# Three hand-written orders of steps laid out anew in a graph-attention kernel

## The chip, the cores and the metric

The kernel runs on one core of one Trainium2 chip. The core has a matrix engine (TensorE; PE in the profile, its weight loads PEld), a vector engine (VectorE, DVE), a scalar engine (ScalarE, ACT), GpSimd (POOL) and a queue that issues transfers (SP). Each engine takes its own instructions in their order; semaphores tie the engines together. The metric is the time of one execution on the device in microseconds, the median of several runs.

## The reference

64 independent graphs of 256 nodes with 512 features each, all in float32, and two layers, each with a residual:

```python
h = jnp.maximum(_layernorm(x, axis=-1), 0.0)
x = x + _L0_gnn_ref(adj, h, W1, att_src1, att_dst1, b1, W2, att_src2, att_dst2, b2)
h = jnp.maximum(_layernorm(x, axis=-1), 0.0)
x = x + _L1_gnn_ref(h, adj, W_proj, W_att, b_att)
```

Layer 0 is two graph attentions with an ELU between them (four heads of 256, then one head of 512), layer 1 is one attention with eight heads of 64 and a ReLU. One attention is

```python
xl = (x @ W).reshape(B, N, H, F)
e = jax.nn.leaky_relu(asrc[:, :, None, :] + adst[:, None, :, :], 0.2)
e = jnp.where(mask[..., None], e, NEG_INF)
attn = jax.nn.softmax(e, axis=1)
out = jnp.einsum('bsdh,bshf->bdhf', attn, xl)
```

where `asrc` and `adst` are dot products of a node's features with two attention vectors.

## The kernel before

**Stages of a graph.** A `Graph` object (from L292) has one method a step. `load` brings x and the adjacency; `masks`, `caps` and `cap3` make the masks of the layers (`cap3` transposes one by two transfers); `bias` adds b2 on GpSimd. `stats1`, `norm1` normalise; `away1` writes h to DRAM and reads it back permuted, and `turn1` finishes its transposition on VectorE and lets GpSimd form four sums (`left`). Then the first projection (`m1a`, `m1b`, two halves of the columns), `exp1`, `rows1`, four `edges1`, four `gat1` (head pair, row block), `out1`, `elu1`. `send2` and `back2` transpose half of the result over DRAM and VectorE, `turn2` the other half on TensorE; second projection `m2`, `exp2`, `rows2`, `edges2`, two `gat2`, `out2`. Layer 1: `stats3`, `norm3`, `turn3` (transposes on TensorE, copies on ScalarE, sums on GpSimd), projection `m3`, `exp3`, `rows3`, eight `edges3`, four `gat3`, `out3`, then `range` and `store`.

**Products.** A projection is a Strassen-like product (L38) of seven block products, `p1` to `p7`, here in the order their operands come; `c22` adds up one block of the result. The first product needs only a block of the input as it is; `p5`, `p6`, `p7`, `p4` need the sums that GpSimd makes (`left`, L212) and the sums of the weights (`right`, L551).

**Attention.** `exp` takes exponentials of the node terms, `rows` (`spread`, L233) transposes them on VectorE, writes them to DRAM and reads them back spread over all partitions (one transfer for `rows2`, two for `rows1`, four for `rows3`, after one small write). `edges` (`weigh`, L286) makes the 256 x 256 weights of one head: per row block a scaling on ScalarE and one operation on VectorE. `gat` is the matmul with the weights; its last column gives the sum by which `out` divides. `gat1` (L394) and `gat2` (L466) use 128-wide weights; `gat3` (L518) issues per head, row block and half 64-wide weights against 65 columns, 16 source matmuls a step, 32 records in the profile.

**The order.** Nothing is scheduled automatically: `run` (L693) goes through a text of steps and issues each, so a text is the order on every engine and queue at once. An item is the graph's offset from the round r, the step and its arguments; items of graphs outside 0 to 63 are left out. `head` runs once, `order` for r = 2 to 62, `tail` once with r = 64. In the order before, round r starts with the `gat1` of graph r and carries parts of the graphs r-2 to r+2; the head ends inside graph 2, with the load of graph 3 last.

**Weights.** The steps `w` of the head prepare weights once: `dots1`, `dots2` (eight steps of four dot products each, L559, on VectorE) and `dots3` (a product on GpSimd, a reduction on VectorE, L629) make the columns for the attention terms; `sums1`, `sums2`, `sums3` the sums of the weights. A product of `m1a` needs the columns that `dots1` writes into `w1a_sb`; `m1b` has none.

**Buffers.** PSUM: four of `ps_mm` (tile pm), two of `ps_sum`, two of `ps_tr`. Nine of e, three of wy, two each of xs, ad, cap and mask, one of h.

```python
    for r in range(2, B - 1):
        run(order, r)
    run(tail, B)
```

Of the kernel before, what the change touches and what calls it, by code (L numbers as in the profile page):

```python
# [97 lines left out]
def short_path(ctx, tc, flags, x, adj, w1, att_src1, att_dst1, b1, w2, att_src2, att_dst2, b2, w_proj, w_att,  # L98
# [487 lines left out]
    class Weights:  # L586
# [49 lines left out]


    head = """
        w dots1 3, w dots1 0, 0 turn0, 0 masks, 0 m1b p1, w dots1 2, w dots1 5, w sums1 1, w dots1 1, 0 m1b
        p2, 0 m1b p6, 0 m1b p7, w dots2 0, 0 m1b p5, w dots1 4, 0 m1b c22, w dots1 6, w dots1 7, 0 m1b p4, 0  # L640
        m1a p1, w sums1 0, 0 m1a p6, w dots2 3, 0 m1a p7, w dots2 2, w dots2 7, w dots2 5, 0 m1a p5, 0 bias,
        0 m1a p2, 0 m1a c22, w dots2 1, 0 m1a p3, 0 m1a p4, w dots2 4, w dots2 6, w columns2, 0 m1b p3, w
        sums2 0, w sums2 1, 0 exp1, 0 rows1, w sums2 2, 0 caps, w sums2 3, 0 edges1 0, 0 edges1 3, 0 edges1
        1, 0 edges1 2, 0 gat1 0 0, w load3, 0 cap3, 0 out1 0 0, 0 gat1 0 1, 0 out1 0 1, 0 gat1 1 0, 0 elu1 0
        0, 0 send2 0, 0 out1 1 0, 0 elu1 0 1, 1 load, 0 send2 1, 0 elu1 1 0, 0 gat1 1 1, 0 back2 0, 0 out1 1
        1, 0 back2 1, w dots3 7, 1 stats1, 1 masks, 0 elu1 1 1, 1 norm1, w dots3 1, 0 m2 p1, w dots3 2, w
        dots3 0, 1 away1, w dots3 6, 0 turn2 0, 0 turn2 1, w dots3 5, 0 m2 p6, w dots3 4, w dots3 3, 1
        turn1, w sums3 0, w sums3 1, 0 m2 p2, w sums3 2, 0 m2 p7, 0 m2 p5, 1 m1a p1, 0 m2 p4, 1 m1a p6, 0 m2
        c22, 0 m2 p3, 1 m1a p7, 1 m1a p5, 0 exp2, 0 rows2, 1 m1a c22, 1 m1b p1, 1 bias, 1 m1a p4, 1 m1a p3,
        1 m1a p2, 1 exp1, 1 rows1, 1 m1b p6, 1 m1b p2, 1 m1b p5, 0 edges2, 1 m1b p7, 1 caps, 0 gat2 0, w  # L650
        sums3 3, 1 m1b c22, 0 out2 0, 0 stats3 0, 1 edges1 0, 1 m1b p3, 0 gat2 1, 1 edges1 1, 0 out2 1, 1
        m1b p4, 1 edges1 2, 1 gat1 0 0, 1 out1 0 0, 0 stats3 1, 2 load, 1 gat1 0 1, 1 out1 0 1, 1 elu1 0 1,
        1 edges1 3, 0 norm3, 1 elu1 0 0, 1 cap3, 1 send2 0, 1 gat1 1 0, 0 turn3, 1 send2 1, 1 out1 1 0, 1
        gat1 1 1, 1 out1 1 1, 2 stats1, 0 m3 p1, 0 m3 p2, 1 elu1 1 0, 1 elu1 1 1, 2 norm1, 1 back2 0, 0 m3
        p6, 0 m3 p5, 1 turn2 0, 1 back2 1, 0 m3 p7, 2 away1, 1 m2 p1, 2 bias, 2 masks, 1 turn2 1, 0 m3 c22,
        1 m2 p2, 0 m3 p4, 0 m3 p3, 0 exp3, 0 rows3, 2 turn1, 1 m2 p6, 1 m2 p5, 1 m2 p7, 2 m1a p1, 1 m2 c22,
        1 m2 p3, 2 m1a p6, 1 m2 p4, 1 exp2, 1 rows2, 0 edges3 1, 2 m1a p5, 2 m1a p7, 2 m1a c22, 0 edges3 2,
        0 edges3 4, 2 m1b p1, 2 m1a p3, 0 edges3 3, 2 m1a p2, 0 edges3 6, 0 edges3 0, 2 m1b p6, 0 gat3 0 1,
        2 m1a p4, 2 m1b p2, 2 exp1, 2 rows1, 2 m1b p5, 0 edges3 5, 0 gat3 0 0, 0 edges3 7, 1 edges2, 2 m1b
        p7, 0 out3 0 0, 0 out3 0 1, 1 gat2 0, 2 caps, 2 m1b c22, 1 out2 0, 1 stats3 0, 2 edges1 0, 2 m1b p3,  # L660
        2 edges1 1, 2 edges1 3, 2 m1b p4, 1 gat2 1, 1 out2 1, 3 load
    """
# [28 lines left out]
    weights = Weights()

# [293 lines left out]
```

## Time and profile before

| | |
|---|---|
| median of 3 runs | 3147.14 us (3146.95 to 3150.41) |
| span of the profiled execution | 3144.0 us |
| TensorE busy | 3064.8 us, 97% |
| PEld, VectorE, ScalarE, GpSimd busy | 84%, 78%, 60%, 40% |
| DMA, mean | 110 GB/s |
| VectorE busy, 0 to 100 us, 100 to 200 us | 69.64 us, 68.66 us |
| VectorE busy, 200 to 300 us | 80.27 us |

"Busy" is the union of the times in which an engine has an instruction. A matmul's end is modelled and matmuls overlap, so on TensorE a full row can still hold short waits; the distance between two starts shows them. In a line of the timeline the first number is the start from the span's beginning in microseconds, the second the busy time, then engine, source line, operation, what is written and read, the shape, and how many instructions were merged; in brackets the idle time before it and what ended it. GpSimd's times are rough.

### The profile page before, as it was taken

What the parts mean: (1) busy time and instruction counts of PE and PEld (TensorE: products, weight loads), DVE (VectorE), ACT (ScalarE), POOL (GpSimd) and SP (SyncE); (2) the same over time, 40 slices, a digit from 0 to 9 for tenths busy, and PEclk for the clock granted to TensorE, in tenths of its full rate; (3) what the DMA queues carried; (4) which work ended last, traced back from release to release, by engine and by line L of the source; (5) the groups of instructions that cost most, each with busy time, mean ns of one, the idle gap of its engine ahead of it and who ended that gap; (6) DMA issues with size and microseconds to landing.
All of it is one profiled execution on the core that took longest, in us unless ns stands there. A gap on an engine that the chain in (4) does not pass through costs nothing. (4 is left out here: it accounts for less than half of the span.)

```text
span 3144.0 us, 60657 instructions
## 1 busy us (share of the span) xinstructions
PE 3064.8 (97%) x21312; PEld 2628.9 (84%) x21312; DVE 2466.5 (78%) x6503; ACT 1882.1 (60%) x4743; POOL 1245.5 (40%) x1434
## 2 busy tenths in 40 slices
PE   4899999999999999999999999999999999999997
PEld 3788888888888888888888888888888888888886
DVE  7588788787787787787787887887887877877875
ACT  2466666665666666566566666566666656666664
POOL 1443433433433434434434434434434334334342
PEclk8999999999999999999999999999999999999999
DMA  4234443333433433434433333433444334334331
GB/s 138 71 110 113 117 107 115 118 108 105 126 102 111 127 102 111 127 100 113 120 106 112 116 106 114 115 109 117 108 116 117 107 109 123 105 108 127 102 112 36
DMA packets 350779, 346.49 MB, mean 110 GB/s; under 512 B 78600, under 2 KB 236168, under 8 KB 350472
## 3 DMA queue, kind: packets, MB, share of 16 engines
q1 hardware_dynamic: 349096, 340.45, 37.6%
q8 instruction: 174, 2.85, 0.4%
q10 hardware_dynamic: 1376, 2.10, 0.2%
q14 instruction: 133, 1.09, 0.1%
HBM read 231.87 MB, written 102.20 MB: 106 GB/s over the span
## 5 line engine op out<-in xcount | busy, mean ns | idle before, releaser
L289 ACT ACTIVATE wy<-bc,exs_sb 128x256 f32<-128x256 f32 x1646 | 731.7, 500 | 261.7 <-DVE e L290 148.3
L260 DVE TENSOR_TENSOR xl<-pm,kept 128x256 f32<-128x256 f32 (+2 forms) x768 | 318.1, 421 | 414.6 <-PE pm L54 395.5
L60 ACT ACTIVATE kept<-sum 128x264 f32<-128x264 f32 (+3 forms) x768 | 294.4, 383 | 419.1 <-PE sum L54 416.2
L394 PE MATMUL pm<-xl,e 128*128 128x257 f32 x2048 | 498.6, 387 | 20.6 <-DVE e L290 15.1
L528 POOL TENSOR_TENSOR x<-x,o 128x256 f32<-128x256 f32 x256 | 196.4, 768 | 788.8 <-DVE o L526 770.2
L54 PE MATMUL sum<-w_sb,h1s 128*128 128x257 f32 x2048 | 489.7, 381 | 7.7 <-POOL h1s L216 7.1
L290 DVE SCALAR_TENSOR_TENSOR e<-wy,exs_sb,cap 128x256 f32<-128x256 f32 x1024 | 446.9, 479 | 56.0 <-ACT wy L289 56.0
L394 PEld LDWEIGHTS pm<-xl,e 128*128 128x128 f32 x2048 | 369.3, 190 | 100.2 <-PE pm L394 28.3
L54 PEld LDWEIGHTS sum<-w_sb,h1s 128*128 128x128 f32 x2048 | 380.6, 191 | 67.1 <-POOL h1s L216 7.5
L54 PE MATMUL pm<-w_sb,h1s 128*128 128x257 f32 x1536 | 365.4, 380 | 1.2 <-DVE xl L260 1.0
L181 POOL TENSOR_TENSOR rstd<-ve,neg_half 128x2 f32<-128x2 f32 x128 | 116.8, 912 | 622.0 <-DVE ve L179 622.0
L54 PEld LDWEIGHTS pm<-w_sb,h1s 128*128 128x128 f32 x1536 | 291.1, 190 | 45.4 <-issue 1.4
L290 DVE SCALAR_TENSOR_TENSOR e<-wy,exs_sb,mask 128x256 f32<-128x256 f32 x640 | 302.4, 523 | 5.2 <-ACT wy L289 5.2
L518 PEld LDWEIGHTS pm<-xl,e 128*64 128x64 f32 x8192 | 250.6, 138 | 47.3 <-issue 22.7
L54 PE MATMUL sum<-w1b_sb,hs 128*128 128x256 f32 x1024 | 266.7, 384 | 7.8 <-DVE w1b_sb L554 5.0
L54 PE MATMUL sum<-w1a_sb,hs 128*128 128x260 f32 x1024 | 268.7, 385 | 5.7 <-DVE w1a_sb L554 3.3
L54 PE MATMUL sum<-wp_sb,hs 128*128 128x264 f32 x1024 | 270.6, 387 | 3.0 <-ACT kept L60 2.5
L518 PE MATMUL pm<-xl,e 128*64 128x65 f32 x8192 | 269.2, 224 | 3.9 <-DVE e L290 2.9
L404 DVE SCALAR_TENSOR_TENSOR z<-pm,r,b_sb 128x256 f32<-128x256 f32 x512 | 247.8, 484 | 18.2
L466 PE MATMUL pm<-xl,e 128*128 128x257 f32 (+1 forms) x1024 | 242.6, 380 | 1.3 <-DVE e L290 1.3
L407 ACT ACTIVATE ez<-z 128x512 f32<-128x512 f32 x256 | 159.8, 624 | 125.0 <-DVE z L404 125.0
L54 PEld LDWEIGHTS sum<-w1b_sb,hs 128*128 128x128 f32 x1024 | 196.7, 193 | 36.9 <-issue 7.0
(103 smaller groups left out, 5076.3 us busy)
## 6 DMA issues: line engine op xcount, KB each, us to landing
bc<-kept SPq DMA_DIRECT2D x380, 256.0 KB
xs<-in_x_dram SPq DMA_DIRECT2D x64, 512.0 KB
out_dram<-x SPq DMA_DIRECT2D x64, 512.0 KB
kept_h<-h SPq DMA_DIRECT2D x63, 512.0 KB
h<-kept_h SPq DMA_DIRECT2D x63, 512.0 KB
kept_z<-z SPq DMA_DIRECT2D x124, 256.0 KB
z<-kept_z SPq DMA_DIRECT2D x124, 256.0 KB
ad<-in_adj_dram SPq DMA_DIRECT2D x64, 256.0 KB
```

Of the source, the lines that this page charges most:

```text
L54: self.nc.tensor.matmul(to[:, :self.n], self.lhs[:, i, c, :], self.rhs[:, i, c, :], start=(first and c == 0), stop=(last and c == self.nk ...
L60: self.nc.scalar.activation(s[:, :self.n], self.sum[:, :self.n], AF.Copy)
L181: nc.gpsimd.tensor_tensor(rstd, ve[:, 0, :], neg_half, ALU.pow)
L260: nc.vector.tensor_tensor(dst, pm, add, ALU.add)
L289: nc.scalar.activation(wy, bc, AF.Copy, scale=yw)
L290: nc.vector.scalar_tensor_tensor(dst, wy, xw, mask, ALU.max, op)
L394: nc.tensor.matmul(pm[:, :Q + 1], self.e[1, h][:, s, t * P:(t + 1) * P], xl1[:, s, h, L1:], start=(s == 0), stop=(s == T - 1))
L404: nc.vector.scalar_tensor_tensor(z[:, sl], pm[:, :Q], r, b1_sb[:, sl], ALU.mult, ALU.add)
L407: nc.scalar.activation(ez, z[:, 2 * g * F1:2 * (g + 1) * F1], AF.Relu, scale=-1.0)
L466: nc.tensor.matmul(pm[:, :n], self.e[2][:, s, t * P:(t + 1) * P], xl2[:, s, half, L2:L2 + n], start=(s == 0), stop=(s == T - 1))
L518: nc.tensor.matmul(pv[q:q + 64, h, :], self.e[3, a * G + h][:, s, t * P + q:t * P + q + 64], xl3[:, s, a * G + h, :], start=(s == 0), stop ...
L528: nc.gpsimd.tensor_tensor(to, to, o.rearrange("p h k -> p (h k)"), ALU.add)
```

## The change

The three texts are replaced; `Graph` gets an initial value for `bc2` and `bc3`, the rows that `rows2` and `rows3` set. Steps, instructions and buffers stay as they are. The round now begins with `edges1 3` of graph r-1 and carries parts of the graphs r-3 to r; the head ends inside graph 1, and the tail carries what is left of the graphs 60 to 63. The line numbers after the first hunk are higher by one.

```diff
@@ -295,6 +295,7 @@
         def __init__(self, b):
             self.b = b
             self.pms = {}
+            self.bc2 = self.bc3 = None
 
         def load(self):
             self.xs = io.tile([P, T, D], F32, name="xs")
@@ -636,57 +637,57 @@
     head = """
-        w dots1 3, w dots1 0, 0 turn0, 0 masks, 0 m1b p1, w dots1 2, w dots1 5, w sums1 1, w dots1 1, 0 m1b
-        p2, 0 m1b p6, 0 m1b p7, w dots2 0, 0 m1b p5, w dots1 4, 0 m1b c22, w dots1 6, w dots1 7, 0 m1b p4, 0
-        m1a p1, w sums1 0, 0 m1a p6, w dots2 3, 0 m1a p7, w dots2 2, w dots2 7, w dots2 5, 0 m1a p5, 0 bias,
-        0 m1a p2, 0 m1a c22, w dots2 1, 0 m1a p3, 0 m1a p4, w dots2 4, w dots2 6, w columns2, 0 m1b p3, w
-        sums2 0, w sums2 1, 0 exp1, 0 rows1, w sums2 2, 0 caps, w sums2 3, 0 edges1 0, 0 edges1 3, 0 edges1
-        1, 0 edges1 2, 0 gat1 0 0, w load3, 0 cap3, 0 out1 0 0, 0 gat1 0 1, 0 out1 0 1, 0 gat1 1 0, 0 elu1 0
-        0, 0 send2 0, 0 out1 1 0, 0 elu1 0 1, 1 load, 0 send2 1, 0 elu1 1 0, 0 gat1 1 1, 0 back2 0, 0 out1 1
-        1, 0 back2 1, w dots3 7, 1 stats1, 1 masks, 0 elu1 1 1, 1 norm1, w dots3 1, 0 m2 p1, w dots3 2, w
-        dots3 0, 1 away1, w dots3 6, 0 turn2 0, 0 turn2 1, w dots3 5, 0 m2 p6, w dots3 4, w dots3 3, 1
...
+        w dots1 2, w dots1 1, w dots1 3, w dots1 0, w dots1 7, w dots1 6, w dots1 4, 0 turn0, w dots1 5, w sums1 0,
+        0 m1a p1, 0 m1a p2, 0 m1a p6, w sums1 1, w dots2 0, 0 bias, 0 m1b p1, 0 m1a p5, 0 m1a p7, 1 load, 0 m1b p5,
+        0 m1a c22, 0 m1a p4, w dots2 7, 0 m1a p3, 0 exp1, 0 masks, 0 rows1, w dots2 3, w dots2 4, w dots2 1,
+        w dots2 2, 0 m1b p6, 0 caps, 0 m1b p7, 0 m1b c22, 1 stats1, 0 edges1 0, 0 m1b p4, 0 m1b p3, 0 edges1 1,
+        0 m1b p2, 0 edges1 3, 0 edges1 2, 0 gat1 0 1, 0 gat1 0 0, 0 out1 0 1, 1 norm1, 0 send2 0, 0 out1 0 0,
+        0 gat1 1 1, w dots2 6, 0 gat1 1 0, 0 elu1 0 1, 0 out1 1 0, 0 elu1 0 0, 0 back2 0, 0 send2 1, 0 out1 1 1,
+        w dots2 5, w columns2, 0 elu1 1 1, 0 elu1 1 0, w load3, 0 back2 1, w dots3 4, 0 cap3, 0 m2 p1, 0 turn2 0,
+        w dots3 7, w sums2 0, 1 away1, w sums2 1, w sums2 2, 1 bias, w dots3 3, 0 turn2 1, 0 m2 p2, 1 turn1,
+        w sums2 3, 0 m2 p5, 0 m2 p6, 1 m1a p1, 0 m2 p7, 1 masks, 0 m2 c22, 1 m1a p6, w dots3 6, 0 m2 p4, w dots3 1,
+        0 m2 p3, 0 exp2, 1 m1a p7, 1 m1a p5, 0 rows2, w dots3 2, 1 m1a c22, w dots3 0, 1 m1a p2, w dots3 5,
+        1 m1a p3, 1 caps, w sums3 0, 1 m1a p4, 1 exp1, 1 m1b p1, 1 rows1, w sums3 1, 1 m1b p5, 0 edges2, 1 m1b p6,
+        0 gat2 0, w sums3 2, 0 out2 0, 0 gat2 1, 0 stats3 0, 0 out2 1, 1 cap3, 1 edges1 0, 1 m1b p7, 0 stats3 1,
+        1 edges1 1, 1 edges1 2, 1 m1b p4, 0 norm3, 1 gat1 0 0, 1 out1 0 0, 1 m1b c22, w sums3 3, 1 m1b p2,
+        1 elu1 0 0
     """
     order = """
-        0 gat1 0 0, 0 edges1 2, 0 out1 0 0, -2 gat3 1 1, 0 cap3, -1 stats3 1, -2 gat3 1 0, -1 norm3, -2 out3
-        1 1, 0 gat1 0 1, 0 elu1 0 0, 0 out1 0 1, 0 gat1 1 0, -1 turn3, 0 out1 1 0, 0 gat1 1 1, 0 elu1 0 1,
-        -1 m3 p1, 0 out1 1 1, 0 elu1 1 0, 0 send2 0, 1 stats1, -1 m3 p5, -1 m3 p6, 0 elu1 1 1, 0 back2 0, 0
-        send2 1, -2 out3 1 0, -1 m3 p2, 1 norm1, 1 away1, 0 back2 1, -2 store, -1 m3 p7, 0 turn2 0, 0 turn2
-        1, 0 m2 p1, -1 m3 p4, -1 m3 c22, 0 m2 p2, -1 m3 p3, 0 m2 p6, 1 masks, -1 exp3, 1 caps, 0 m2 p5, 1
-        bias, -1 rows3, 0 m2 p7, -2 range, 1 turn1, 1 m1a p1, 0 m2 p4, 0 m2 c22, 0 m2 p3, -1 edges3 1, 0
-        exp2, 0 rows2, 1 m1a p6, -1 edges3 0, 1 m1b p1, -1 edges3 5, 1 m1a p7, 1 m1a p5, 1 m1a c22, -1
-        edges3 4, 1 m1a p2, -1 edges3 2, 1 m1a p4, 1 m1a p3, -1 edges3 3, 1 exp1, 1 m1b p6, 1 rows1, -1
-        edges3 7, -1 gat3 0 0, -1 gat3 0 1, -1 out3 0 0, 0 edges2, -1 edges3 6, 1 m1b p5, -1 out3 0 1, 1 m1b
-        p7, 1 m1b c22, 1 m1b p2, 0 gat2 0, 0 out2 0, 0 stats3 0, 1 edges1 0, 1 m1b p3, 1 edges1 1, 1 m1b p4,
-        0 gat2 1, 0 out2 1, 1 edges1 3, 2 load
+        -1 edges1 3, -1 gat1 0 1, -2 turn3, -3 out3 1 1, -1 out1 0 1, -1 m1b p3, -2 m3 p1, 0 load, -1 gat1 1 0,
+        -1 gat1 1 1, -1 out1 1 0, -1 send2 0, -1 elu1 0 1, -2 m3 p6, -1 out1 1 1, 0 stats1, -2 m3 p5, -2 m3 p7,
+        -1 send2 1, -1 back2 0, 0 norm1, -1 elu1 1 1, -1 elu1 1 0, -3 gat3 1 0, -2 m3 p4, -2 m3 c22, -2 m3 p2,
+        -1 back2 1, -1 turn2 0, -1 turn2 1, 0 masks, -2 m3 p3, 0 away1, -3 range, -2 exp3, -1 m2 p1, -2 rows3,
+        0 caps, -3 out3 1 0, 0 turn1, -1 m2 p5, -1 m2 p6, -1 m2 p2, -1 m2 p7, -1 m2 c22, 0 m1a p1, -2 edges3 1,
+        -2 edges3 3, -1 m2 p4, -1 m2 p3, -1 exp2, 0 m1a p6, -1 rows2, -2 edges3 0, 0 bias, -3 store, 0 m1a p5,
+        -2 edges3 7, 0 m1a p7, 0 m1a c22, -2 edges3 2, 0 m1a p2, -2 edges3 5, 0 m1a p4, 0 m1a p3, -1 edges2,
+        -2 gat3 0 0, 0 exp1, 0 m1b p1, -2 out3 0 0, 0 rows1, -1 gat2 0, -2 edges3 6, -1 out2 0, -1 gat2 1,
+        -2 edges3 4, -1 stats3 0, -1 out2 1, 0 m1b p6, -1 stats3 1, -2 gat3 0 1, 0 edges1 0, 0 m1b p7, 0 m1b p2,
+        0 edges1 1, 0 edges1 2, -1 norm3, 0 m1b p4, 0 gat1 0 0, 0 out1 0 0, 0 m1b p5, -2 out3 0 1, 0 m1b c22,
+        0 elu1 0 0, 0 cap3, -2 gat3 1 1
     """
     tail = """
...
-        edges3 2, 0 m1b p5, -2 edges3 4, 0 exp1, 0 m1b p2, -2 edges3 6, -2 gat3 0 0, -2 gat3 0 1, 0 m1b p6,
-        -2 out3 0 1, 0 m1a p2, -2 range, -1 edges2, -2 edges3 7, -2 edges3 5, -1 gat2 0, 0 rows1, 0 m1a c22,
-        -1 out2 0, -1 gat2 1, -1 stats3 0, -2 gat3 1 0, -1 out2 1, -1 stats3 1, -1 norm3, -1 turn3, -2 out3
-        0 0, -2 gat3 1 1, -1 m3 p1, -2 out3 1 1, 0 m1a p4, -1 m3 p2, -1 m3 p5, -1 m3 p6, -1 m3 p7, -1 m3 p4,
-        -1 m3 c22, -2 out3 1 0, -1 m3 p3, -1 exp3, -1 rows3, -1 range, -1 edges3 4, -1 edges3 6, -1 edges3
-        1, -1 edges3 0, -1 edges3 3, -1 edges3 2, -1 edges3 5, -1 edges3 7, -2 store, -1 gat3 0 0, -1 gat3 0
-        1, -1 gat3 1 1, -1 out3 0 1, -1 gat3 1 0, -1 out3 0 0, -1 out3 1 1, -1 out3 1 0, -1 store
...
+        -2 m3 p2, -3 gat3 1 1, -3 range, -2 m3 p5, -3 out3 1 1, -1 turn2 0, -1 turn2 1, -2 m3 p7, -3 store,
+        -2 m3 c22, -1 m2 p1, -2 m3 p3, -2 m3 p4, -2 exp3, -1 m2 p6, -1 m2 p5, -1 m2 p7, -2 rows3, -1 m2 c22,
+        -2 edges3 1, -1 m2 p2, -2 edges3 3, -2 edges3 5, -4 range, -2 edges3 0, -1 m2 p3, -2 edges3 6, -1 m2 p4,
+        -1 exp2, -1 edges2, -1 gat2 0, -1 gat2 1, -2 edges3 2, -1 out2 0, -1 stats3 0, -1 out2 1, -2 gat3 0 1,
+        -1 stats3 1, -2 gat3 0 0, -2 edges3 7, -2 edges3 4, -2 out3 0 0, -2 gat3 1 0, -1 norm3, -1 turn3,
+        -2 out3 1 0, -1 m3 p1, -2 range, -2 gat3 1 1, -1 m3 p6, -1 m3 p2, -1 rows2, -1 m3 p7, -1 m3 p5, -1 m3 p4,
+        -1 m3 c22, -1 m3 p3, -1 exp3, -2 out3 0 1, -2 out3 1 1, -1 edges3 6, -2 store, -1 edges3 5, -1 edges3 4,
+        -1 edges3 7, -1 edges3 0, -1 edges3 3, -1 edges3 1, -1 gat3 1 1, -1 edges3 2, -1 gat3 1 0, -1 gat3 0 1,
+        -1 out3 1 0, -1 out3 1 1, -1 out3 0 1, -1 gat3 0 0, -1 out3 0 0, -1 range, -1 store
     """
```

## The prediction

> **What bounds it now.** I read the totals first, then the stretches, then TensorE's own order of events, and last the waits at the start. The chain of waits on the page reaches back over less than one per cent of the span, so it carries nothing here.
>
> ```profile
> span 3144.0 us, 60657 instructions
> PE 3064.8 (97%) x21312; PEld 2628.9 (84%) x21312; DVE 2466.5 (78%) x6503; ACT 1882.1 (60%) x4743; POOL 1245.5 (40%) x1434
> ```
>
> ```profile
> 0.00:100.00 100.00, 53.93 (x191) 41.33 (x192) 69.64 (x226) 25.12 (x55) 32.34 (x45) 0.86 0.38 115
> 100.00:200.00 100.00, 92.55 (x539) 77.72 (x538) 68.66 (x180) 57.05 (x147) 34.36 (x41) 1.00 0.35 102
> 200.00:300.00 100.00, 99.82 (x743) 86.00 (x742) 80.27 (x211) 63.26 (x163) 38.55 (x44) 1.00 0.38 109
> ...
> 3100.00:3144.00 44.00, 27.63 (x334) 22.19 (x332) 23.07 (x73) 16.26 (x42) 9.30 (x14) 0.89 0.07 26
> ```
>
> The columns are stretch, length, busy time of PE, PEld, DVE, ACT and POOL, granted clock, DMA share, GB/s. TensorE is idle 53.5 us in the first 200 us (46.1 and 7.4), 16.4 us in the last 44, and 0.2 in a hundred between. So the rounds are bound by TensorE, and a new order can win there only what hides inside "busy": matmuls overlap, so I go by the distance from one start to the next.
>
> ```profile
> 155.15 1.89 PE L54 MATMUL pm<-w1b_sb,hs 128*128 128x256 f32 x8
> 156.97 1.15 PE L518 MATMUL pm<-xl,e 128*64 128x65 f32 x32
> 158.06 1.13 PE L54 MATMUL sum<-w1b_sb,hs 128*128 128x256 f32 x4
> 159.02 1.89 PE L466 MATMUL pm<-xl,e 128*128 128x257 f32 x8
> ```
>
> ```profile
> 1009.57 1.03 PE L54 MATMUL sum<-w1b_sb,hs 128*128 128x256 f32 x4
> 1010.52 2.09 PE L518 MATMUL pm<-xl,e 128*64 128x65 f32 x64
> 1012.54 1.13 PE L54 MATMUL pm<-w1b_sb,hs 128*128 128x256 f32 x4
> 1013.51 1.03 PE L54 MATMUL sum<-w1b_sb,hs 128*128 128x256 f32 x4
> 1014.37 1.03 PE L54 MATMUL pm<-w1b_sb,hs 128*128 128x256 f32 x4
> ...
> 1020.42 1.90 PE L394 MATMUL pm<-xl,e 128*128 128x257 f32 x8
> 1022.25 2.09 PE L518 MATMUL pm<-xl,e 128*64 128x65 f32 x64
> 1024.26 4.06 PE L394 MATMUL pm<-xl,e 128*128 128x257 f32 x16
> 1028.16 1.04 PE L196 MATMUL pt<-ident,h 128*128 128x128 f32 x8
> ```
>
> Each line gives a start and a busy time; one source matmul of the wide kind is two records. Four wide records take 0.86 us (1013.51 to 1014.37), eight 1.73, wherever they stand; an m2 product 1.74, an m3 product 0.89. The reader is to see two things. First, a run of the 64-wide matmuls of `gat3` has edges: before the run at 156.97, eight records take 1.82 us instead of 1.73, and after it four take 0.96 instead of 0.86. Second, the sixteen records from 1024.26 take 3.90 us, where sixteen take 3.46 and the edge 0.10: the other 0.33 us is a wait inside `gat1 1 0`, behind a VectorE that runs `out1`, `stats3` and `out3` without a break from 1022.97 to 1029. The round is 47.51 us long (a run begins at 202.86 and, 17 rounds on, at 1010.52).
>
> **The change, part by part: the runs of gat3.** No instruction is added, so TensorE's work could only change at edges. The round before has `gat3 0 0, gat3 0 1` and `gat3 1 1, gat3 1 0` side by side on TensorE (the steps between the last two do not use it). The round after has all four apart: `gat3 0 0` between `m1a p3` and `m1b p1`, `gat3 0 1` between `m1b p6` and `m1b p7`, `gat3 1 1` between `m1b p5` and the next round's `gat1 0 1`, `gat3 1 0` between `m3 p7` and `m3 p4`. Counting the instructions as built, runs of 64-wide matmuls rise from 129 to 251: 122 more. The price: two runs of 32 cost 2 x (0.09 + 1.09 + 0.10) = 2.56 us, one run of 64 costs 0.09 + 2.02 + 0.11 = 2.22. A split costs 0.34 us, and nothing hides it, as it is on the engine that sets the end. 122 x 0.34 = 41.5 us. The row at 156.97 is the only undisturbed single run. From below: the outer edges alone, 0.20 a split (24 us). From above: the other single run of the start, from 152.90 to 154.17, which holds a wait of its own, in place of one of the two: 0.09 + 1.27 + 0.12 + 1.28 - 2.22 = 0.54 (66 us). I take 0.34, as the outer edges of the long runs agree with the row.
>
> The Trainium skill ("TensorE: Matmul & The Clock Gate", Part 3, the span model) gives packed small matmuls about 4 ns of issue each and prices no edge; Part 2 there says that weight loads are pulled ahead of running matmuls. By it the 122 splits would cost about half a microsecond, an estimate from that page, and the sum below would be some 41 us lower. The row shows the edge, and the row decides.
>
> **The wait that goes.** In the new round `m1b p3` and `m3 p1` (0.86 + 0.89 us of TensorE) stand between `gat1 0 1` and `gat1 1 0`, and `stats3` has moved ahead of the round's end, so VectorE's work ahead of `out1 0 1` is `edges1 3` (0.80) and `out3 1 1` (0.55) against 2.6 us of `gat1 0 1` and `turn3`. The 0.33 us should go: 61 rounds x 0.33 = 20 us less. If it stays, add those 20 back.
>
> **The waits that come.** A cover has got thinner at `gat2 0`. Its e comes over `m2 p3`, `exp2`, `rows2`, DMA, `edges2`. In the old order two `gat3` and some ten products lie between; in the new one only six m1a products, `gat3 0 0` and `m1b p1`: 6 x 0.88 + 1.28 + 0.86 = 7.4 us. The chain: eviction 0.4, exponentials 0.4, the transpose and DMA 5.7, weighing 1.3, together 7.8. The 5.7 is from these rows:
>
> ```profile
> 1058.40 0.20 DVE L237 STREAM_TRANSPOSE wt<-exs_sb 128x32 f32<-128x32 f32 x1
> ...
> 1064.12 1.30 ACT L289 ACTIVATE wy<-bc,exs_sb 128x256 f32<-128x256 f32 x3 [1.67 <-DMA bc<-kept]
> ```
>
> That is `rows1`, with two transfers; `rows2` has one of half the size, so 5.7 is its upper side, and what it saves is unknown. TensorE keeps order: all behind `gat2 0` waits with it, `gat2 1` first, and on VectorE `out2 0`. Next, `gat1 0 0`: from the end of `gat2 0` TensorE has `gat2 1`, four m1b products and `gat3 0 1`, 1.73 + 3.44 + 1.28 = 6.45 us, while VectorE has `out2` twice (2.1), `edges3 4` (0.8), `stats3` (1.95), one eviction (0.35) and `edges1 0, 1` (1.6) = 6.8 us and may start 0.7 us earlier, at the first half of `gat2 0`: 0.35 us to spare. `m2 p5` wants the first sum that GpSimd makes after `turn2`'s copies, which queue on ScalarE behind `norm1` as in the old round; to spare, about nothing. On SP `cap3` now waits for the last `edges3` of two graphs earlier (two buffers of cap), and the load behind it for `cap3`; 8.6 us of TensorE's steps to the round's end and 8 more to `stats1`, less 2.5 for `cap3`, leave the load 14 us, and the first load of the program (issued at 0.80, used at 6.79) took 6. `away1`'s two transfers may hold VectorE at `turn1` (write and read took 7.4 us there: issued at 1037.29, used at 1044.66) with a microsecond left before `m1a p1`. So per round 0 to 0.8 us; I take 0.25, near the first of these waits: 61 x 0.25 = 15 us.
>
> **The start.**
>
> ```profile
> 11.65 0.43 DVE L559 CUSTOM_DVE_ANT_0 wy<-w1b_sb,x 128x256 f32<-128x256 f32 x1 [2.88 <-DMA w1b_sb<-in_L_gnn_W_dram]
> ...
> 19.72 2.55 DVE L559 CUSTOM_DVE_ANT_0 wy<-w1a_sb,x 128x256 f32<-128x256 f32 x1
> 22.20 2.86 DVE L554 TENSOR_TENSOR w1b_sb<-w1b_sb 128x512 f32<-128x512 f32 x4
> ```
>
> A dot starts every 0.35 us, but every 0.87 beside GpSimd's `left` and 2.5 beside `bias`. The new head puts all 32 of `dots1` first: 11.65 + 18 dots up to 22.2 (as the rows run) + 14 x 0.35 = 27.1 us to the first m1a product, where m1b began at 15.7. That is 11 us later, in a time in which TensorE mostly waited. Afterwards only 24 of 32 `dots2` come before `edges1`, and neither `columns2` nor `sums2`: 27.1 + sums1 5.7 + dots2 8.3 + evictions, masks and stats1 about 4.5 + waits 1.5 = 47 us, where `edges1` began at 57.95. And TensorE's 3.2 us before 74.64 and 7.1 before 82.75, the latter behind GpSimd with ten of `dots3`'s sixteen products ahead of `left`, shrink: now six of them stand ahead. To the end of the new head VectorE has 64 dots (22.2 us), the subtractions (14.1), `dots3` (5.6), graph 0's steps (19.7) and graph 1's (11.5), 73 us, and TensorE 51 (m1 23.5, m2 12.2, `gat1` 8.6, `gat2` 3.5, turns 2.9); from 11.65 on, with 5 us of slowing by GpSimd, that ends at 90 us at the earliest and leaves TensorE idle for 39, against 53.5. I take 10 us won, between 0 (the late first product costs all) and 15.
>
> **The end.** After the last `gat2` the chain over `norm3`, m3, `exp3`, eight `edges3`, `out3` and the store is the same; four rather than two `gat3` of the graph before fill it (2 us), and two more `edges3` stand ahead of `norm3` on ScalarE (2 x 0.8 us). I take nothing, plus or minus 3.
>
> **Sum** against the profiled span: 3144.0 + 41.5 - 20 + 15 - 10 = 3170.5 us. The median of the runs shown is 3147.1, 3.1 above that span; with that, 3174 us.
>
> **Rivals.** *The round gets waits of a microsecond.* For it: margins of 0.35 and 0 us, and VectorE's pieces cost up to twice as much beside GpSimd, as `bias` does at 19.72. Against: VectorE is 80% busy and catches up each round. At 1.0 us a round: 3147.1 + 41.5 - 20 + 61 - 10 = 3220. *A split is cheaper*, 0.20 us, because the inner edge overlaps elsewhere: 3147.1 + 24 - 20 + 15 - 10 = 3156; for it, only one run of 32 was seen. *The start wins, and the change is faster.* This is the one with the other sign: the order of VectorE's weight work in the head saves so much idle time of TensorE that it outweighs the splits. Its price is the start's 53.5 us of idle time; without any new wait the rounds lose 41.5 - 20 = 21.5 us, and from there on it decides. At 30 us saved: 3139. For it, the 10.3 us of waits before 82.75 and `edges1` 11 us earlier; against it, the first product at 27 us and the VectorE bound of 15.
>
> **How the numbers follow.** The forecast (splits near 0.34, new waits under 0.6) has 0.62 and its own range is 3155 to 3198; the many waits 0.15, the cheap split 0.13, the start 0.10. The low end is all that is favourable inside the forecast: 3147.1 + 41.5 - 20 - 15 - 3 = 3150; below it lie the start's case and little else. The high end, 3204, is 0.75 us of waits a round and takes in half of the many waits. A measurement of this kernel tells about 0.2% (6.3 us) from no change. Faster: 0.09, from the start's case; within 0.2% (3141 to 3153): 0.10, from the cheap split with a good start; slower: 0.81.
>
> **What would show it.** In the profile after: runs of 32 at line 519 with 0.09 before, 1.09 in and 0.10 after each, four a round; a round of 48.1 us instead of 47.5; sixteen records of `gat1` no longer in 3.90; a wait at the `gat2` matmuls of 0 to 0.8; in the first 200 us TensorE idle some 43 us. I am wrong if the single run is cheaper between other neighbours, if the round is under 47.6, or if the start saves more than 22.

## The result, and the profile after

The kernel became slower: 3221.46 us, the median of four runs (3215.09 to 3235.86), against 3147.97 for the kernel before on the same chip. The ratio is 1.0239, with a 95% interval of 1.0213 to 1.0265. The profiled execution of after took 3215.09 us, 6 less than the median, so the traces account for 68.9 us (spans 3212.9 and 3144.0) of the 73.5 between the medians. The four runs of after spread over 21 us, those of before over 3.5.

First the totals of after, then the same stretches as before (length, busy time of PE, PEld, DVE, ACT, POOL, granted clock, DMA share, GB/s).

```profile
span 3212.9 us, 60227 instructions
PE 3132.8 (98%) x21312; PEld 2612.3 (81%) x21312; DVE 2549.7 (79%) x6503; ACT 1854.4 (58%) x4743; POOL 1177.5 (37%) x1434
```

```profile
0.00:100.00 100.00, 66.03 (x270) 52.29 (x271) 81.88 (x264) 37.22 (x85) 35.54 (x50) 0.95 0.43 134
100.00:200.00 100.00, 98.34 (x644) 82.21 (x643) 78.93 (x200) 58.98 (x151) 36.99 (x46) 1.00 0.35 104
200.00:300.00 100.00, 98.31 (x670) 81.86 (x669) 79.05 (x201) 58.06 (x150) 36.49 (x45) 1.00 0.36 107
...
1000.00:1100.00 100.00, 98.67 (x672) 82.61 (x671) 79.43 (x200) 58.11 (x151) 37.67 (x47) 1.00 0.36 108
```

The 430 instructions fewer than before are all waits on semaphores; every engine has as many instructions of its work as before. Two opposite effects stand here. In the first 200 us TensorE is busy 164.4 us instead of 146.5: the start is better by 18. In the middle it is 98.3 or 98.7% busy where it was 99.8: the rounds now hold idle time that even the union of the busy times shows. A share of 1.1 to 1.5% of some 2900 us of rounds would be 30 to 45 us. That is not all, since a wait shorter than what is left of a matmul's modelled end does not show as idle time.

So I measured TensorE the way the prediction read it: the distance from each start to the next, less the usual distance of that class (0.216 us for a wide record, 0.093 more before a run of `gat3` and 0.104 more after one). What is left is waiting. By stretch of the span, in us:

| | before | after |
|---|---|---|
| 0 to 200 us | 58.7 | 36.6 |
| 200 to 3000 us | 24.5 | 74.3 |
| 3000 us to the end | 18.0 | 17.2 |
| all waits | 101.2 | 128.0 |
| runs of `gat3` | 129 | 251 |

The waits grow by 26.8 us; 122 runs more at 0.347 us are 42.3. Together that is 69.1, against 68.9 between the two spans. The two terms have to add up, since a wait is here whatever the usual distances and edges leave over; that the edges cost what is assumed is shown by `b_split` below. The question is where the 50 us of new waits in the rounds come from. The round is 49.05 us long in the mean instead of 47.55, and varies between 48.4 and 50.5; before, 48 of 56 rounds took 47.5.

The waits that the page lists (what waited, for what; us in total, times, longest) give the first hint. Before:

```profile
ACT wy L289 <- DMA bc<-kept: 76.7, 53, 8.0
```

After:

```profile
ACT wy L289 <- DMA bc<-kept: 145.9, 99, 3.2
...
PEld sum L54 <- ACT kept L60: 60.5, 115, 1.9
```

ScalarE waits twice as often for the rows that come back from DRAM, and TensorE's weight loads wait 115 times for `kept`, ScalarE's copy of a product's running sum (before: 2.1 us, 2 times). The timeline of one round shows how the two hang together; lines of PE, ACT, DVE and SP, with waits in brackets.

```profile
1062.24 0.32 SPq L244 DMA_DIRECT2D bc<-kept  x1
...
1065.24 0.91 ACT L289 ACTIVATE wy<-bc,exs_sb 128x256 f32<-128x256 f32 x2 [0.91 <-DMA bc<-kept]
...
1066.06 0.39 ACT L284 ACTIVATE exs_sb<-xl 128x8 f32<-128x8 f32 x3
...
1067.21 0.20 DVE L237 STREAM_TRANSPOSE wt<-exs_sb 128x32 f32<-128x32 f32 x1
...
1069.41 0.80 SPq L244 DMA_DIRECT2D bc<-kept  x2
...
1072.05 1.13 PE L54 MATMUL sum<-w1b_sb,hs 128*128 128x256 f32 x4
...
1072.95 0.91 ACT L289 ACTIVATE wy<-bc,exs_sb 128x256 f32<-128x256 f32 x2 [1.50 <-DMA bc<-kept]
1073.02 1.03 PE L54 MATMUL pm<-w1b_sb,hs 128*128 128x256 f32 x4
...
1073.77 0.36 ACT L60 ACTIVATE kept<-sum 128x256 f32<-128x256 f32 x1
...
1074.18 1.13 PE L54 MATMUL sum<-w1b_sb,hs 128*128 128x256 f32 x4
```

Read it from the top. The rows of `rows2` are asked for at 1062.24; `edges2` holds ScalarE until they have landed, to 1065.24. Only behind it, in ScalarE's order, come the exponentials of `exp1` (1066.06), and with them the second trip over DRAM, `rows1` (1067.21 to 1072.95): two trips, one after the other. The first weighing of `edges1 0` waits for this second trip, and the order puts it ahead of `m1b p7`'s copy. `m1b p7` began at 1072.05. In `a_kept` and `a_rows1` below its copy begins 1.17 us after it in every round, which would be 1073.22 here; it begins at 1073.77. `m1b p4` adds on to the same sum and cannot start before the copy has read it: 1.16 us after `m1b p2` instead of 0.86. In all 51 rounds between 400 and 2900 us this weighing starts 83 or 84 ns after the first transfer of `rows1` has landed, so it is the transfer that it waits for; and from round to round the wait at `m1b p4` follows the length of that trip (correlation 0.98 over 50 rounds).

A weighing that waits for its rows is no loss by itself. Before, the first weighing of `edges1 0` also starts 83 or 84 ns after the landing in 50 of 52 rounds, but there the copy of `m1b p7` stands ahead of it, and no product of `m1b` waits. What is new is the copy behind the weighing.

### The profile page after: what moved, and what is told of

Same layout as the page of the kernel before. It is cut to its first block, busy times and chain, and to the rows that moved or that the text cites. A ratio compares the mean times of both kernels' runs of the same rounds, so it can differ in the third digit from the quotient of the medians.

```text
span 3212.9 us, 60227 instructions
## 1 busy us (share of the span) xinstructions
PE 3132.8 (98%) x21312; PEld 2612.3 (81%) x21312; DVE 2549.7 (79%) x6503; ACT 1854.4 (58%) x4743; POOL 1177.5 (37%) x1434
## 3 DMA queue, kind: packets, MB, share of 16 engines
q14 instruction: 131, 1.07, 0.1%
## 5 line engine op out<-in xcount | busy, mean ns | idle before, releaser
L289 ACT ACTIVATE wy<-bc,exs_sb 128x256 f32<-128x256 f32 x1646 | 720.8, 498 | 276.2 <-DMA bc<-kept 145.9
L290 DVE SCALAR_TENSOR_TENSOR e<-wy,exs_sb,cap 128x256 f32<-128x256 f32 x1024 | 556.0, 594 | 98.3 <-ACT wy L289 97.5
L395 PE MATMUL pm<-xl,e 128*128 128x257 f32 x2048 | 481.9, 383 | 1.2 <-DVE r L403 0.8
L395 PEld LDWEIGHTS pm<-xl,e 128*128 128x128 f32 x2048 | 382.9, 189 | 59.5 <-PE pm L395 1.4
L519 PEld LDWEIGHTS pm<-xl,e 128*64 128x64 f32 x8192 | 259.5, 137 | 86.1 <-issue 85.2
L290 DVE SCALAR_TENSOR_TENSOR e<-wy,exs_sb,mask 128x256 f32<-128x256 f32 x640 | 279.4, 486 | 56.9 <-ACT wy L289 55.8
L181 POOL TENSOR_TENSOR rstd<-ve,neg_half 128x2 f32<-128x2 f32 x128 | 97.6, 763 | 592.4 <-DVE ve L179 592.3
L54 PE MATMUL sum<-w1b_sb,hs 128*128 128x256 f32 x1024 | 283.2, 399 | 24.8 <-ACT kept L60 24.1
L519 PE MATMUL pm<-xl,e 128*64 128x65 f32 x8192 | 294.9, 225 | 1.4 <-DVE e L290 1.2
L54 PEld LDWEIGHTS sum<-w1a_sb,hs 128*128 128x128 f32 x1024 | 185.5, 190 | 69.4 <-issue 32.5
```

The lines of the kernel that those rows point to most:

```text
L54: self.nc.tensor.matmul(to[:, :self.n], self.lhs[:, i, c, :], self.rhs[:, i, c, :], start=(first and c == 0), stop=(last and c == self.nk ...
L181: nc.gpsimd.tensor_tensor(rstd, ve[:, 0, :], neg_half, ALU.pow)
L289: nc.scalar.activation(wy, bc, AF.Copy, scale=yw)
L290: nc.vector.scalar_tensor_tensor(dst, wy, xw, mask, ALU.max, op)
L395: nc.tensor.matmul(pm[:, :Q + 1], self.e[1, h][:, s, t * P:(t + 1) * P], xl1[:, s, h, L1:], start=(s == 0), stop=(s == T - 1))
L519: nc.tensor.matmul(pv[q:q + 64, h, :], self.e[3, a * G + h][:, s, t * P + q:t * P + q + 64], xl3[:, s, a * G + h, :], start=(s == 0), stop ...
```

## The experiments

All places that wait in the rounds, in us a round, means over 50 rounds of each trace (a wait counts with the 0.05 to 0.10 us that the next record loses behind it). "Rest" is the round's length less all waits. The table is worked out from the traces; the runs follow below. A trace is one execution: it took 6 us less than the median in after, 9 less in a_kept, within about 3 of it in the other rows, so a few microseconds between two times say nothing.

| | m1b p4 | m1a p7 (p4 where named) | m2 p6 (p7) | gat2 0 | gat1 0 0 | round | rest | time |
|---|---|---|---|---|---|---|---|---|
| after | 0.59 | 0.25 | 0.23 | 0.13 | 0 | 49.05 | 47.86 | 3221 |
| a_kept | 0 | 0.23 | 0.22 | 0.23 | 0.19 | 48.76 | 47.89 | 3207 |
| a_rows1 | 0 | 0.31 | 0.22 | 0.34 | 0 | 48.74 | 47.87 | 3191 |
| a_both | 0 | 0.35 | 0.22 | 0.34 | 0.19 | 48.95 | 47.85 | 3204 |
| a_waits | 0 | 0.78 (p4) | 0.76 (p7) | 0.07 | 0.19 | 49.71 | 47.92 | 3250 |
| a_cover | 0 | 0.05 | 0.22 | 1.29 | 0.19 | 49.64 | 47.90 | 3244 |
| a_laid | 0 | 0 | 0.22 | 0.64 | 0.44 | 49.20 | 47.90 | 3219 |

The rest is the same for all orders with four parted runs of `gat3`. For before it is 47.55 - 0.37 = 47.18: two splits a round, 0.69 us, separate the two kinds of order, and everything else is waits.

The three places on the left of the table are of one kind: a product that adds on to a running sum waits for ScalarE's copy of that sum. At `m2 p6` this is seen in the round at 1049 us of after (ScalarE's exponentials of `exp3`, its copy of the sum of `m2 p1`, then `m2 p6`; in the first line the second of GpSimd's sums, which `m2 p6` also needs):

```profile
1047.36 1.33 POOL L216 TENSOR_TENSOR h1s<-h1s 128x512 f32<-128x512 f32 x1
...
1048.76 0.32 ACT L500 ACTIVATE exs_sb<-lg 128x16 f32<-128x16 f32 x2 [0.81 <-DVE lg L495]
...
1048.98 0.37 ACT L60 ACTIVATE kept<-sum 128x257 f32<-128x257 f32 x1
...
1049.49 0.89 PE L54 MATMUL sum<-w_sb,h1s 128*128 128x257 f32 x3
```

GpSimd's sum is ready at 1048.69, 0.8 us earlier; the copy, which stands behind `exp3` in ScalarE's order, ends at 1049.35, and `m2 p6` starts 0.14 us after it, in all 50 rounds between 0.143 and 0.145. At `m1b p4` the distance from the copy's end is 0.052 or 0.053 us in all 50 rounds, and `m1a p7` starts 0.14 us behind the copy of `m1a p6`'s sum, which stands behind `exp2`, in the 30 rounds in which it waits. These three make 1.07 of the 1.19 us.

**The split alone.** The order of before, with the two pairs of `gat3` taken apart:

```diff
-0 cap3, -1 stats3 1, -2 gat3 1 0, -1 norm3, -2 out3 1 1, 0 gat1 0 1, 0 elu1 0 0
+0 cap3, -1 stats3 1, -1 norm3, -2 out3 1 1, 0 gat1 0 1, -2 gat3 1 0, 0 elu1 0 0
...
--1 gat3 0 0, -1 gat3 0 1, -1 out3 0 0, 0 edges2, -1 edges3 6, 1 m1b p5, -1 out3 0 1
+-1 gat3 0 0, -1 out3 0 0, 0 edges2, -1 edges3 6, 1 m1b p5, -1 gat3 0 1, -1 out3 0 1
```

> The kernel before, with the pairs of gat3 of its round apart (gat3 0 1 behind m1b p5, gat3 1 0 behind gat1 0 1) and nothing else moved: 251 runs instead of 129. If a run's edges cost 0.347 us each time, the 122 new runs add 42 us: 3190. If the edge was particular to the one single run seen in the start, or is hidden between other neighbours, the time stays at 3148 to 3160.

Measured: 3169.98 us, ratio 1.0068 (1.0051 to 1.0085). The total was missed by 20 us, and the trace says why. TensorE in one round:

```profile
1032.50 1.15 PE L518 MATMUL pm<-xl,e 128*64 128x65 f32 x32
1033.59 2.00 PE L394 MATMUL pm<-xl,e 128*128 128x257 f32 x8
1035.52 1.15 PE L518 MATMUL pm<-xl,e 128*64 128x65 f32 x32
1036.60 2.00 PE L394 MATMUL pm<-xl,e 128*128 128x257 f32 x8
```

The reader is to see a run of 32 take 1.08 to 1.09 us from start to start of the next group, and the eight records between two runs 1.93 (1033.59 to 1035.52), which is 1.73 + 0.10 + 0.09. So a split costs what was predicted. But `gat3 1 0` now stands between `gat1 0 1` and `gat1 1 0` and gives VectorE its time: the old 0.33 us wait is gone, and waits from 200 to 3000 us fall from 24.5 to 3.7. 42.3 - 20.7 = 21.6, as measured (21.2 us above before's median on that chip). So a round with four parted runs can be all but free of waits (3.7 us in 2800).

**The copy behind the weighing.** The order of after, with `0 edges1 0` moved behind `0 m1b p7`, so that the copy stands ahead of the weighing on ScalarE.

> The changed kernel with edges1 0 issued behind m1b p7 instead of ahead of it, so that ScalarE copies p7's sum before it waits for the rows of edges1 0. Theory K (ScalarE's queue: the copy stands behind a weighing that waits for rows1's transfer, and m1b p4 waits for the copy): the wait before m1b p4 (0.59 us a round) goes, 36 us less, about 3185. Rival V (VectorE comes late, and the wait only shows first at p4): the wait turns up again at gat1 0 0, and the time stays within 10 us of 3221.

Measured: 3206.95 us, ratio 1.0193 (1.0176 to 1.021), 14.5 us under after. The wait at `m1b p4` went completely, as the table shows, and about half of it came back: `gat1 0 0` wants the weights that now come later (0.19 in every round), and `gat2 0` rose by 0.10. Neither expectation holds as it was written; that the copy stood behind the weighing is shown, since the wait at `m1b p4` went with this one move.

**The runs joined again.** The order of after, with `gat3 0 0` moved down to `gat3 0 1`, `gat3 1 0` up to `gat3 1 1`, and their `out3` after them.

> The changed kernel with gat3 0 0 moved to gat3 0 1 and gat3 1 0 to gat3 1 1, their out3 with them: runs of 64 again, 129 instead of 251. If edges cost 0.347 us a run: 42 us less, about 3179, with the waits of the round (1.2 us) left as they are. If the waits take the place of the edges (something else than TensorE sets the round's length, VectorE above all): within 15 us of 3221.

Measured: 3334.08 us, ratio 1.0602 (1.0572 to 1.0631), far from both. The rest came down to 47.18 as it should, but waits rose to 3.8 us a round: 1.47 at `gat2 0`, 0.75 at `m3 p4`, 0.75 at `m1a p7`, 0.6 in `gat1 0 1`. Here is the second of them:

```profile
1023.52 1.05 PE L54 MATMUL sum<-wp_sb,hs 128*128 128x264 f32 x4
1025.05 1.16 PE L54 MATMUL sum<-wp_sb,hs 128*128 128x264 f32 x4 [0.48 <-ACT kept L60]
```

These are `m3 p7` and `m3 p4`. With `gat3 1 0` between them nothing waited; side by side the second starts 1.53 us after the first instead of 0.89. `m1a p7` waits for a copy too, 0.144 us behind its end in all 50 rounds. So the two parted runs that were moved are not only a cost: `gat3 1 0` covers the wait at `m3 p4`, and `gat3 0 0` that at `gat2 0`. The wait in `gat1 0 1` was not followed up.

**The new head on the old round.** The order of before, its first graphs begun as in after (the head of after as far as it goes, then what the old head still has to do).

> The kernel before with the changed kernel's head, followed by the steps of the old head that it leaves out in their old order; round and end as before. From the traces, TensorE's waits in the first 200 us fell from 58.7 to 36.6 us, of which 2.6 us of rounds in either: if that is the head's own, 22 us less, about 3126. If the new head only fits the new round, the seam gives it back: 3140 or more.

Measured: 3130.46 us, ratio 0.9946 (0.993 to 0.9963): 18 us won. The stretches at the start:

```profile
0.00:100.00 100.00, 66.05 (x260) 51.94 (x260) 81.34 (x262) 35.11 (x80) 34.77 (x48) 0.93 0.43 133
100.00:200.00 100.00, 94.24 (x600) 78.83 (x600) 70.80 (x181) 56.92 (x146) 34.87 (x40) 0.98 0.31 90
```

VectorE is busy 81 us of the first hundred instead of 70, and TensorE 66 instead of 54. TensorE is idle for 39.7 us of the first 200, about the 39 that the prediction had as the least; only 10 of the gain had been counted.

**The old head on the new round**, as the counterpart: after, its first graphs in the order of before.

> The kernel after with the first graphs in the order of before (the steps of the new head, sorted as the old head had them); round and tail as after. Theory (head, round and tail add up, as the head alone gave before 18 us): 3221 + 18 to 22 = 3239 to 3243. Rival (the gain of the head is partly owed to what the round after it waits for, as the new round starts inside graph 1): within 8 us of 3221, or over 3255.

Measured: 3240.07 us, ratio 1.0302 (1.0278 to 1.0325), 18.6 us above after, and 23.4 between the two profiled executions: within the spread of after's runs, head and round add up.

**The second trip earlier.** The order of after, with `exp1` and `rows1` ahead of `edges2`:

```diff
-0 m1a p4, 0 m1a p3, -1 edges2, -2 gat3 0 0, 0 exp1, 0 m1b p1, -2 out3 0 0, 0 rows1, -1 gat2 0
+0 m1a p4, 0 m1a p3, 0 exp1, 0 rows1, -1 edges2, -2 gat3 0 0, 0 m1b p1, -2 out3 0 0, -1 gat2 0
```

> The changed kernel with exp1 and rows1 issued ahead of edges2, so that the exponentials do not stand on ScalarE behind the weighing that waits for rows2's transfer; the transposition for rows1 then starts some 1.5 us earlier, its rows land as much earlier. Theory D (two trips over DRAM in a chain, rows2 to edges2 to exp1 to rows1 to edges1 0): the wait before m1b p4 falls from 0.59 us a round to under 0.2, edges2 pays up to 0.2 at gat2 0, so 12 to 30 us less than 3221: 3190 to 3209. Rival V (VectorE is behind): within 8 us of 3221.

Measured: 3191.05 us, ratio 1.0141 (1.012 to 1.0161): 30 us won by two items in the text. The list of waits:

```profile
PEld pm L467 <- DVE e L290: 30.5, 62, 1.1
PEld sum L54 <- ACT kept L60: 14.4, 56, 1.7
ACT wy L289 <- DMA bc<-kept: 12.8, 12, 3.7
```

ScalarE's waits for rows fall from 145.9 us to 12.8, and 99 times to 12; the weight loads' waits for `kept` from 60.5 to 14.4. The 0.59 us at `m1b p4` are gone. What came instead is the first line: `gat2 0` waits for its e, which comes after `exp1` now, 0.34 us a round instead of 0.13. The transposition of `rows1` begins 2.08 us after `m1a p3` instead of 3.94 (means over 50 rounds), and its rows land as much earlier. With a_kept this shows the cause of the wait at `m1b p4`: the weighing was late because one trip over DRAM waited for the other in ScalarE's order, and the copy stood behind the weighing. Of the 30 us between the medians 24 stand between the two profiled executions.

**Four moves at once.** After with the two moves above, and `m2 p2` put ahead of `m2 p6`, `m1a p2` ahead of `m1a p7`, to give the products that were seen to wait there more time.

> The changed kernel with four swaps: edges1 0 behind m1b p7, exp1 and rows1 ahead of edges2, m2 p2 ahead of m2 p6 (p6 waits 0.23 us a round for GpSimd's second sum), m1a p2 ahead of m1a p7 (p7 waits 0.25 for ScalarE's copy of p6's sum, behind exp2). The runs of gat3 stay apart. If these queue positions are what the round loses: the waits fall from 1.19 to some 0.3 us a round, the round to 48.15 us, 54 us less than 3221: about 3167. If VectorE's load sets the round: above 3195.

Measured: 3249.92 us, ratio 1.0321 (1.0304 to 1.0338), 83 us above what was expected. TensorE, `m2 p6` and `m2 p7`:

```profile
1009.51 1.90 PE L54 MATMUL sum<-w_sb,h1s 128*128 128x257 f32 x8
1011.93 1.98 PE L54 MATMUL sum<-w_sb,h1s 128*128 128x257 f32 x8 [0.52 <-issue]
```

Both swaps removed the wait that they were meant for and put two products of one running sum side by side: `m2 p6, p7` start 2.42 us apart instead of 1.74, and `m1a p7, p4` likewise. That gives the price of an uncovered copy: 0.76 us (0.68 and 0.07 in the record after), 0.78 at `m1a`. `p2` had been the cover. The expectation took the wait at `m2 p6` for one on GpSimd's second sum; it is one on a copy, as shown above, and the swap removed it because `p2` gave the copy time.

**The two moves together**, without the swaps.

> The round after with two of the moves together: exp1 and rows1 ahead of edges2, and edges1 0 behind m1b p7. In the run with four moves the places that these two touch waited 0.08 + 0.10 us (gat1 0 0) and 0.07 us (gat2 0), while 1.54 us a round came from two pairs of products with nothing between them: m2 p6 before m2 p7 (0.68 + 0.07) and m1a p7 before p4 (0.68 + 0.10). Theory (each wait belongs to its own place: a copy of the running sum that nothing covers costs about 0.76 us): with the two pairs as they were the round is 49.71 - 1.54 + 0.23 + 0.27 = 48.67 us, and the time 3187, between 3180 and 3194. Rival (the copies had nothing to do with it; the round waits because VectorE's and ScalarE's work of a round, moved closer, ends later): the round stays over 49.3 and the time over 3220.

Measured: 3204.26 us, ratio 1.0178 (1.0161 to 1.0195). The 1.54 us of the two pairs are gone, which confirms their price, but the sum is 0.28 us a round above what was expected: `gat2 0` and `m1a p7` wait as in a_rows1, not as in a_waits, where TensorE came to them later.

**A cover for each copy.** The kernel a_both, with `m1a` as p5, p2, p7, c22, `gat3 0 0`, p4, p3 (and `edges3 2`, which `gat3 0 0` reads, ahead of p2).

> The kernel a_both with m1a laid out so that a piece of TensorE's work covers each copy: p5, p2, p7, c22, gat3 0 0, p4 instead of p5, p7, c22, p2, p4. Theory (place by place): the 0.27 to 0.3 us that m1a p7 waited for the copy of p6 behind exp2 go, and p4 has gat3 0 0 (1.28 us) as cover for a copy of 0.76; with no other wait 3187 - 61 x 0.28 = 3170, between 3163 and 3178. Rival (total wait is set by the slower engines' round and only moves from place to place): within 4 us of a_both. If p4 after gat3 0 0 still shows 0.5 us or more, the price of the pair was not the copy.

Measured: 3243.93 us, ratio 1.0306 (1.0289 to 1.0323). Of both waits in `m1a` 0.05 us is left, but 1.29 us stand at `gat2 0`:

```profile
1024.28 1.04 PE L54 MATMUL pm<-w1a_sb,hs 128*128 128x260 f32 x4
1025.16 1.03 PE L54 MATMUL sum<-w1b_sb,hs 128*128 128x256 f32 x4
1025.36 0.43 DVE L260 TENSOR_TENSOR xl<-pm,kept 128x260 f32<-128x260 f32 x1 [0.36 <-PE pm L54]
1025.83 0.41 ACT L284 ACTIVATE exs_sb<-xl 128x8 f32<-128x8 f32 x3 [0.96 <-DVE xl L260]
...
1026.14 0.89 ACT L289 ACTIVATE wy<-bc,exs_sb 128x256 f32<-128x256 f32 x2
1026.66 0.88 DVE L290 SCALAR_TENSOR_TENSOR e<-wy,exs_sb,mask 128x256 f32<-128x256 f32 x2 [0.38 <-ACT wy L289]
...
1027.20 3.73 PE L467 MATMUL pm<-xl,e 128*128 128x257 f32 x16 [1.02 <-DVE e L290]
```

From the start of `m1a p3` (1024.28) over its eviction, `exp1`, a weighing and e to `gat2 0` (1027.20) are 2.92 us; TensorE has 1.74 us of work there (`m1a p3`, `m1b p1`), and 2.92 - 1.74 = 1.18, to which the next record adds 0.11. `gat3 0 0`, taken away to cover a copy, had been the cover of this chain.

**Both covers.** The kernel a_rows1, with `m1a` as p5, p2, p7, c22, `m1b p1`, p4, p3, and `m1b p6` ahead of `gat2 0`.

> The kernel a_rows1 (3191 us) with its two largest remaining waits covered at once: m1a in the order p5, p2, p7, c22, m1b p1, p4, p3 (a cover of two products for the copy of p6, one of 0.86 us for the copy of p7, which takes about 0.76 from end to end), and m1b p6 ahead of gat2 0, so that gat3 0 0 and one product (1.28 + 0.86 us) still stand between m1a p3 and gat2 0. Theory (a wait has a place and a cover, and what went wrong in a_cover is that gat3 0 0 no longer stood ahead of gat2 0): the waits of a_rows1 at m1a p7 (0.22 + 0.05 + 0.04) and at gat2 0 (0.24 + 0.1, if the chain from m1a p3 is no longer than there) shrink to under 0.3 together; 3191 - 61 x 0.35 to 0.65 = 3151 to 3170. Rival (the sum of the waits is set by how much VectorE and ScalarE have to do, and any cover taken from one place is missing at another): 3185 or more, with the wait at m1b p7, p4 or gat1 0 0.

Measured: 3219.44 us, ratio 1.023 (1.0213 to 1.0247): the rival's time. No wait to speak of is left in `m1a`, but `gat2 0` waits 0.64 us, since the eviction of `m1a p3` queues on VectorE behind four operations of `edges3` (1014.07 to 1015.67 in the round at 1014 us), and `gat1 0 0` 0.44, since the two products taken forward no longer cover the trip of `rows1`. ScalarE's wait for rows is back:

```profile
ACT wy L289 <- DMA bc<-kept: 162.5, 67, 3.6
```

The rival's reason, that the amount of work on VectorE and ScalarE sets the sum of the waits, is not shown by this: the sum rose from 0.87 to 1.30 us a round, and b_split, with the same steps in the old order, has almost none.

**The best of both.** The kernel b_head, with `elu1 0 0` behind `out1 0 1`, so that VectorE evicts before it finishes the ELU.

> The kernel before with the changed kernel's head (as b_head, 3130), and in its round elu1 0 0 issued behind out1 0 1. VectorE then frees a PSUM buffer 0.6 us earlier, and the wait of 0.33 us inside gat1 1 0 should go without parting the runs of gat3: 20 us less, about 3110. If the wait is for something else: 3130.

Measured: 3122.99 us, ratio 0.9917 (0.9901 to 0.9934), the fastest of all, 25 us under before. The 0.33 us wait went completely; waits of 0.24 us a round came at other places (`turn3`, twice in `m2`, before `m1a`), so the round is 47.42 us long, 0.13 shorter than before and 0.10 shorter than in b_head, not 0.33. Of the 20 us expected, 7.5 came (3130.46 to 3122.99).

## Why the prediction was wrong

The direction was right; the time lies 17 us above the end of the range. By the steps of the sum:

- *Runs of `gat3`*, +41.5: right. 122 runs more as counted, 0.347 us each, +42.3; the split alone showed it. The estimate that was set against the row, from the 4 ns of issue a matmul in the Trainium skill ("TensorE: Matmul & The Clock Gate", Part 3), was half a microsecond for all of them; the runs decide for the row. The rival of a cheap split falls.
- *The wait that goes*, -20: right. No wait is left in `gat1 1 0`; b_split, where it went too, measured it as 20.7 us.
- *The waits that come*, +15: this step failed. They are 1.2 us a round and about 70 us in all, and the bound of 0.8 a round was too low as well. Of the places named only `gat2 0` came (0.13); `gat1 0 0`, `m2 p5`, the load on SP and `turn1` did not hold up TensorE. The rest, 0.59 at `m1b p4`, 0.25 at `m1a p7` and 0.23 at `m2 p6`, is of a kind that the step put at nothing: it asked of each matmul when its operands come, and not when ScalarE's copy of a running sum is done, which the next product of the same sum waits for. It also followed `rows2` to `gat2 0` as a chain of its own, and did not see that `exp1` and `rows1` had moved behind `edges2` on ScalarE, which put a second trip over DRAM behind the first. In the order before, `rows1` stands ahead of `edges2`. a_rows1 shows that these two items cost 30 us (24 by the traces) of the 55 too much.
- *The start*, -10, bounded at -15: the mechanism was right, the size was not: -22 by the waits, -18 and -18.6 by the two runs with exchanged heads. The first `m1a` product came at 26.5 us (27.1 in the prediction), but the first weighing already at 43.3 instead of 57.4 (47 in the prediction), and after the first product no wait of TensorE in the first 200 us is longer than 2.9 us, where before five are between 3.4 and 7.3 and one is 11.4. The 39 us that TensorE was to be idle at the least were 35.6. The granted clock explains little of it: the throttle gave half clock for 27 us of the start before and for 10 after, and in these stretches at most 5.6 and 3.9 us of the waits can be slower matmuls.
- *The end*, 0 plus or minus 3: right (-0.8).

Put right, the sum is 3144.0 + 42.3 - 20.7 + 70.5 - 22.1 - 0.8 = 3213.2 us, against a span of 3212.9; its terms are taken from the two traces, so it only divides what was measured. The rival "waits of a microsecond a round" gave 3220 and was the case, though by a mechanism that it did not name: it spoke of thin margins and of VectorE beside GpSimd, and 1.07 of the 1.19 us are copies late in ScalarE's order. That its time lies within 2 us of the median is partly luck: the waits were 10 us more than it took and the start won 12 more. The rival of the winning start had a gain of the right kind, but its condition, no new wait in the rounds, did not hold.

VectorE beside GpSimd did get slower, and by more than the "twice" of the prediction, whose own row at 19.72 has 2.55 us for a dot of 0.42. In the new order `bias` falls beside the weighings of `edges3`: 60 of them, about one a round, take 1.5 to 2.6 us instead of 0.48, each beside `bias`, and none did before. VectorE is busy 83 us longer for the same instructions (2549.7 instead of 2466.5). What this adds to the waits is open, as no run moved `bias`.

What stays open is whether the new round can be free of waits. None of its layouts tried had less than 0.87 us a round, and a cover moved to one place was missed at another; that this must be so was not shown, and the four parted runs do not force it, as b_split shows.

## What to carry to other kernels

When steps are reordered, walk through the queue of every engine, not only through the operands of the busiest: ask of each copy that frees a sum or a buffer what now stands ahead of it, and whether that waits for a transfer. Two trips over DRAM that share an in-order engine become one long trip as soon as the first one's consumer is put ahead of the second one's producer. A piece of work that looks like a cost in the wrong place may be the cover of a wait, so price its removal with the wait that it uncovers.

## What the runs showed of the hardware

- The edges of a run of 64-wide matmuls, 0.093 us before and 0.104 after it, were alike wherever the run stood: with them counted as work and not as waits, the round's rest is 47.85 to 47.92 us in all seven layouts of the table, and 47.85 in b_split.
- A product that follows another on the same running sum, with ScalarE's copy between them and nothing to cover it, loses 0.75 to 0.78 us (`m2 p7` and `m1a p4` in a_waits, `m3 p4` in a_join), though the copy itself takes 0.37 to 0.39.
- From the issue of the write to the landing of the first read, the trip over DRAM took 4.9 us in the median for `rows2` and 5.45 for `rows1`, with a tenth of the trips above 5.2 and 5.95; the rounds of after vary with it, and its waits at `m1b p4` reach from 0.18 to 1.7 us.
- With TensorE busier at the start, its granted clock in the first 100 us was 0.93 to 0.97 in after, b_head and b_best, and 0.80 to 0.86 in before, b_split and a_oldhead.
- A weighing of 256 columns on VectorE took 0.48 us with nothing on GpSimd beside it (862 of the 1024 of `edges3` in after, all 1024 before), and 1.5 to 2.6 us beside GpSimd's addition of 1024 columns (`bias`), 60 times in after.
